# Four fifths of a layer's end moved from the turn between two batches to beside the last scans

## The chip, the cores and the metric

One core of one Trainium2 chip. TensorE is PE (its weight loads PEld), VectorE is DVE, ScalarE is ACT, GpSimd is POOL, SyncE is SP. The granted clock is the share of TensorE's full speed that the profile records as allowed.

## The reference, cut to what matters

Four images of 48 x 48 tokens with 128 channels. Layer 0 is a group norm, an input projection to 256 + 256 channels, a depthwise convolution, a selective scan in four directions, and the "layer's end": layer norm over 256 channels, gate, output projection, residual. Layer 1 is attention over the 2304 tokens and then an STU (a causal convolution with 16 spectral filters, and 2 x 16 matrices that are a mixture of four sets).

```python
xz = einsum('bhwc,ec->bhwe', _gn(x), in_proj_w); xin, z = split(xz, 2)
xc = silu(conv(xin) + conv_b)
xs = stack([rows, columns, rows reversed, columns reversed])        # 4 directions, L = 2304
... dt, B, C from xs
h = h * exp(dt*A) + (dt*u)*B;  y = sum_n h*C                        # scan, d = 256, n = 16
y = sum of the four directions, put back in order of rows
y = (y - mu) * rsqrt(var + 1e-5) * norm_g + norm_b                  # over 256 channels
x = x + (y * silu(z)) @ out_proj_w.T                                # the layer's end
t = x; t = t + attention(_ln_t(t)); t = t + stu(_ln_t(t))
```

## The kernel before

One batch is a **scan stage** and a **turn**. The scan stage is 4 directions x 6 chunks of 384 positions; a chunk is 8 "units" (2 halves of the channels x 4 quads of states), so 192 units. Per unit, ACT makes four exponentials, DVE four scans, POOL the product with C, PE the sum over states (y) and the spreading of B over partitions, and DVE or POOL the input product.

```python
# order of the chunks: rows, columns, rows reversed, columns reversed
order = [(k, c) for k in range(K) for c in (range(NCH) if k < 2 else reversed(range(NCH)))]
...
def scans(b, chunks, preps, front, sp, back, work, work_cols):
    total = len(chunks) * CHUNK_COLS + work_cols        # matmul columns of the stage
    def more(share):
        while done[0] < share * total:                  # filler: STU of batch b-1,
            cols = next(work, None)                     # for batch 0 the mixture
            if cols is None: break
            done[0] += cols
    for s in range(len(units) + 2):
        enter(s)                                        # input product s = rep * B
        units[s].scan(0, back.psa); units[s - 1].times_c(); units[s].scan(1, back.psa)
        prepare(s)                                      # a step of the next chunk's preparation
        more((s + 0.5) / len(units))
        spread(s + 2)                                   # B of a coming unit, on PE
        units[s].scan(2, back.psa); units[s].scan(3, back.psa)
        ...
        units[s - 2].sum_c(back.psy)                    # y, on PE
        more((s + 1) / len(units)); prepare(s)
```

PE takes its instructions in this order. The mixture, the filler of batch 0, loads its matrices where it uses them:

```python
def mixture(pool, ps):                                  # pool.two: two buffers
    for k in range(KF):
        M = [pool.two.tile(...) for j in range(2)]
        for t, src in zip(M, ("M_phi_plus", "M_phi_minus")):
            nc.sync.dma_start(t, a[src][:, k].rearrange("i d e -> d i e"))
        ... matmuls on M, yielding after each
```

The layer's end works on five pieces of the tokens (four of 512, one of 256) in pipelined stages, after all scans, with the attention's first slots and a part of the next batch's prologue beside it:

```python
def means(J):    # PE: mean over channels; ACT: zr = Silu(zr)
def center(J):   # DVE: v = v - mu (PSUM), twice; ACT: square
def gate(J):     # DVE: v = v * zr (both in SBUF), twice; POOL: sum of squares
# then: project and variance (PE), add to the residual T (DVE), layer norm to xn (DVE, ACT, POOL),
#       transposes to xnT (PE, ACT)

for b in range(B):
    scans(b, ...)                                        # scan stage
    for i, J in enumerate(epilogue(b, ...)):             # layer's end
        if i % 2 and parts: parts.pop(0)()               # prologue of batch b+1
        if J is not None: next(at) ...                   # attention slots of that piece
    for i in range(slots - BEGIN): next(at); ...         # attention, prologue
    ...                                                  # exp/ln table; first chunk of batch b+1
# after the last batch: its STU alone
```

## Time and profile before

7157.76 us, median of 3 runs (7152.87 to 7163.85). The span of the profiled run is 7140.9 us. A scan stage runs from the batch's first scan to its last y product, a turn from there to the next batch's first scan (the last turn: to the first transfer of the last STU).

| before, us | batch 0 | 1 | 2 | 3 |
|---|---|---|---|---|
| scan stage | 1073.7 | 1343.8 | 1349.3 | 1333.5 |
| last y product to first attention score | 86.7 | 86.8 | 87.9 | 71.9 |
| turn | 308.2 | 308.3 | 309.5 | 236.1 |

The rows below are the view of engine busy time by stretch of the kernel before: stretch and length, then busy time and records of PE, PEld, DVE, ACT and POOL, then the granted clock, the DMA share and GB/s.

```profile
126.90:1200.60 1073.70, 800.85 (x3085) 326.02 (x3085) 949.57 (x980) 642.72 (x1196) 930.54 (x425) 0.75 0.55 132
1508.80:2852.60 1343.80, 1271.18 (x5777) 728.68 (x5777) 1075.96 (x1305) 617.95 (x1177) 932.81 (x424) 0.98 0.68 174
2604.00:2852.60 248.60, 226.88 (x1289) 151.83 (x1289) 166.16 (x212) 85.33 (x172) 149.34 (x65) 0.93 0.60 168
```

Length is PE busy plus PE idle, and that sum is used throughout. Batch 1's stage is 1271 busy + 73 idle at a clock of 0.98: PE-bound. Batch 0's has PE at 75% and DVE and POOL at 87 to 88%. The last row, the end of batch 1's stage, is PE-bound like the rest: PE is busy 227 of 249 us there and DVE 166.

### The profile page before, as it was taken

The page shows a single profiled execution, that of the slowest core. Times are in us where ns is not written, and L with a number is a line of the kernel's source. Part 1 is how long each engine was busy: PE and PEld are TensorE (multiplying, and loading weights), DVE is VectorE, ACT ScalarE, POOL GpSimd, SP SyncE. Part 2 cuts the span into 40 slices and gives each one's busy share as a digit, 9 for nine tenths or more (in the row PEclk, how much of TensorE's full clock was granted, in tenths as well). Part 3 has the DMA queues.
Part 4 walks back from the last instruction along what each step waited for, and adds up shares of the span by engine and source line. Part 5 has one row for each costly group of instructions (what it writes and reads, how often), then busy time and mean ns, then how long its engine had stood idle before and what let it go on. Part 6 is the DMA issues. An engine that isn't in the chain of part 4 may idle for free. (4 is left out here: it accounts for less than half of the span.)

```text
span 7140.9 us, 79677 instructions
## 1 busy us (share of the span) xinstructions
PE 6335.6 (89%) x26760; PEld 3652.2 (51%) x26760; DVE 4863.0 (68%) x6145; ACT 2986.6 (42%) x5616; POOL 3849.3 (54%) x1815
## 2 busy tenths in 40 slices
PE   4777776888999998778999999788999999789999
PEld 2333333434555565534555556534555556547788
DVE  6898897557888876457888886447888887522111
ACT  3666664334445543334454543234454544231000
POOL 2888886036777765126677775205677776300000
PEclk7777777899999999899999999899999999899999
DMA  3555553046777765135767776125676777215545
GB/s 95 139 136 137 135 140 98 22 116 151 177 180 187 190 186 166 37 89 138 173 183 181 189 186 194 44 60 139 168 181 175 196 181 205 83 41 139 159 139 177
DMA packets 648922, 1019.14 MB, mean 143 GB/s; under 512 B 93849, under 2 KB 506649, under 8 KB 623778
## 3 DMA queue, kind: packets, MB, share of 16 engines
q1 hardware_dynamic: 642816, 1010.84, 54.3%
q8 instruction: 213, 3.49, 0.2%
q10 hardware_dynamic: 5698, 3.21, 0.2%
q14 instruction: 195, 1.60, 0.1%
HBM read 895.86 MB, written 117.84 MB: 142 GB/s over the span
## 5 line engine op out<-in xcount | busy, mean ns | idle before, releaser
L456 POOL TENSOR_TENSOR s<-s,bc 128x1536 f32<-128x1536 f32 x768 | 2645.1, 3445 | 260.5 <-DVE s L447 160.2
L447 DVE TENSOR_TENSOR_SCAN s<-dA,carry,s 128x384 f32<-128x384 f32 x2560 | 2440.0, 1001 | 253.5 <-ACT dA L444 251.8
L444 ACT ACTIVATE dA<-rep,A 128x384 f32<-128x384 f32 x3072 | 1753.1, 584 | 973.9 <-DVE s L447 956.2
L939 PE MATMUL cv<-tt,u 128*128 128x256 f32 (+4 forms) x7680 | 1686.6, 359 | 59.4 <-DVE U L959 39.8
L939 PEld LDWEIGHTS cv<-tt,u 128*128 128x128 f32 (+1 forms) x7680 | 1272.3, 191 | 670.2 <-issue 335.7
L959 DVE TENSOR_TENSOR U<-cv,Q 128x256 f32<-128x256 f32 (+1 forms) x1280 | 494.0, 392 | 1035.5 <-PE cv L939 1021.6
L439 POOL TENSOR_TENSOR s<-rep,bc 128x1536 f32<-128x1536 f32 x288 | 993.3, 3449 | 97.7 <-DMA bc<-bcd 97.7
L939 PE MATMUL cv<-tt,us 128*128 128x256 f32 (+4 forms) x3840 | 870.7, 363 | 78.9 <-DVE U L959 41.0
L439 DVE TENSOR_TENSOR s<-rep,B 128x1536 f32<-128x1536 f32 x480 | 834.5, 1739 | 100.6 <-PE B L431 84.6
L464 PE MATMUL y<-s,csum 128*32 128x384 f32 x6144 | 716.2, 541 | 169.1 <-POOL s L456 154.4
L939 PEld LDWEIGHTS cv<-tt,us 128*128 128x128 f32 (+1 forms) x3840 | 637.3, 192 | 321.5 <-issue 96.2
L948 ACT COPY Q<-cv 128x256 f32<-128x256 f32 (+3 forms) x640 | 224.0, 351 | 1377.9 <-PE cv L939 1242.3
L997 PE MATMUL pr<-U,G 128*128 128x512 f32 (+4 forms) x2048 | 717.6, 482 | 48.7 <-DMA G<-gd 40.5
L455 POOL COPY carry<-s 128x4 f32<-128x4 f32 x640 | 120.5, 188 | 1132.9 <-DVE s L447 1049.5
L431 PE MATMUL B<-xd,spread 32*128 32x384 f32 x960 | 475.0, 576 | 18.0 <-DVE s L439 18.0
L447 DVE TENSOR_TENSOR_SCAN s<-dA,s 128x384 f32<-128x384 f32 x512 | 457.1, 940 | 39.2 <-ACT dA L444 37.8
L997 PEld LDWEIGHTS pr<-U,G 128*128 128x128 f32 x2048 | 339.0, 194 | 251.6 <-issue 147.8
L464 PEld LDWEIGHTS y<-s,csum 128*32 128x32 f32 x6144 | 125.5, 111 | 603.4 <-issue 301.8
L700 PE MATMUL s<-xnT 128*128 128x512 f32 (+1 forms) x720 | 356.0, 580 | 51.8 <-ACT e L702 28.5
L702 ACT ACTIVATE e<-s,shift 128x512 f32<-128x512 f32 (+1 forms) x360 | 231.4, 644 | 335.2 <-PE s L700 335.0
L161 POOL TENSOR_TENSOR ln_vu<-ln_vu,mhalf 128x4 f32<-128x4 f32 (+1 forms) x20 | 31.4, 1571 | 623.1 <-DVE ln_vu L160 623.1
L693 PE MATMUL o<-e,xn 128*128 128x512 f32 (+1 forms) x720 | 340.2, 556 | 0.0
(167 smaller groups left out, 4883.4 us busy)
## 6 DMA issues: line engine op xcount, KB each, us to landing
rep<-dtdud SPq DMA_DIRECT2D x768, 384.0 KB, 7.8
tt<-fd SPq DMA_DIRECT2D x192, 577.0 KB, 4.2
bc<-bcd SPq DMA_DIRECT2D x2304, 48.0 KB, 3.7
tt<-fd SPq DMA_DIRECT2D x192, 513.0 KB, 4.2
tt<-fd SPq DMA_DIRECT2D x192, 385.0 KB, 3.8
dtdud<-re SPq DMA_DIRECT2D x768, 96.0 KB, 2.2
G<-gd SPq DMA_DIRECT2D x192, 256.0 KB, 4.8
tt<-fd SPq DMA_DIRECT2D x64, 514.0 KB, 5.4
```

The costliest lines, as they stand in the source:

```text
L431: nc.tensor.matmul(self.bt[:, :CS], spread[32:64, self.q].rearrange("p c j -> p (c j)"), self.ch.xd[32:64], start=True, stop=True)
L439: eng.tensor_tensor(s, self.ch.rep[self.h][:, 1], bt.unsqueeze(1).to_broadcast([P, G4, CS]), ALU.mult)
L444: nc.scalar.activation(dA[:, :CS], ch.rep[self.h][:, 0, g], AF.Exp, scale=A[:, ch.k, self.h * G4 + g, self.q:self.q + 1])
L447: nc.vector.tensor_tensor_scan(s, dA[:, CS - 1::-1] if ch.rev else dA[:, :CS], s, 0.0 if ch.first else carry[:, self.h, self.q, g:g + 1], ...
L456: nc.gpsimd.tensor_tensor(self.s, self.s, ch.bc[Q4 + self.q].unsqueeze(1).to_broadcast([P, G4, CS]), ALU.mult)
L464: nc.tensor.matmul(ch.y[g * DL:(g + 1) * DL, :CS], csum, self.s[:, g], start=(self.q == 0), stop=(self.q == Q4 - 1))
L693: nc.tensor.matmul(po[J][:, :w], xn[:, i], e[:, :w], start=(i == 0), stop=(i == NT - 1))
L700: nc.tensor.matmul(p[:, :w], xnT[:, i * P:(i + 1) * P], xnT[:, 512 * J:512 * J + w], start=True, stop=True)
L702: nc.scalar.activation(e[:, :w], p[:, :w], AF.Exp, bias=shift)
L939: nc.tensor.matmul(p2[:, :, at - first:], x, t[:kp, :, hi - 1 - at + J * P:end if end >= 0 else None:-1], start=(J == 0), stop=(J == nb - 1))
L959: nc.vector.tensor_tensor(dst, src, q, ALU.add)
L997: nc.tensor.matmul(p[:, :, :v], Gs[n][:, q, x, :], U[n][:, 4 * q:4 * q + 4, :v], start=False, stop=(k == KF - 1 and q == 1 and v == w))
```

## The change

Intent: the turn begins with the layer's end, in which PE idles and no other engine is full. If the last direction is the one along the rows, backwards, then the rows are complete from the end as its chunks finish, and four of five pieces (the last rows first) could be done while the last scans still run. Their buffers are taken not to fit beside the STU's, so the STU (the mixture for batch 0) is issued within the first 84% of the units, its buffers are freed, and the pieces come after it. Silu is replaced by tanh in the prologue, to stay in one table set.

```diff
-    order = [(k, c) for k in range(K) for c in (range(NCH) if k < 2 else reversed(range(NCH)))]
+    order = [(k, c) for k in (0, 1, 3, 2) for c in (range(NCH) if k < 2 else reversed(range(NCH)))]
 # prologue, for z:
-                    nc.scalar.copy(t, now["ps"][:, :SUB])
+                    nc.scalar.activation(t, now["ps"][:, :SUB], AF.Tanh)      # win's z half is halved
+                    nc.vector.scalar_tensor_tensor(t, t, 1.0, now["ps"][:, :SUB], ALU.add, ALU.mult)
 # scans:
+    WORK_END = 0.84
-        total = len(chunks) * CHUNK_COLS + work_cols
+        total = WORK_END * len(chunks) * CHUNK_COLS + work_cols
-            while done[0] < share * total:
+            while done[0] < share / WORK_END * total or share > WORK_END:
                 cols = next(work, None)
                 if cols is None:
+                    late(complete[0])                  # one step of the pieces
                     break
+        def add_y(u):                                  # notes down to which row y is complete
 # epilogue() becomes class Finish, piece(J) a generator of 11 to 12 steps:
 #   load z, T | mean | centre, square | gate, sum of squares | project 0, variance |
 #   rsqrt, project 2 | add 0 | add 2, norm | norm | norm | transpose | copy
+        def steps():
+            for J in range(NM - 1, 0, -1):             # pieces 4, 3, 2, 1; piece 0 in the turn
+                while now[0] > 512 * J // CS: yield
+                for _ in fin[b].piece(J, bank, vbank): yield
 # attention starts with what is ready:
-        pieces = [0, 4, 1, 2, 3]
+        pieces = [1, 4, 2, 3, 0]
+        keys = [*range(PIECES[0], NT), *range(PIECES[0])]
 # (cut: PSUM and SBUF pools, piece 0 interleaved with attention, exp_tanh() at the turn)
```

## The prediction

> **What bounds the kernel now.** One batch is one scan stage (24 chunks of 384 positions times 8 quads, 192 "units", with the previous batch's STU as PE filler; the mixture of the STU's matrices as filler for batch 0), then one "turn" (the layer's end in five pieces, attention, the prologue of the next batch). After the last turn the last STU runs alone. I read the engine shares by slice first, then cut the span at the first scan and the first mean matmul of each batch in the view of engine busy time by stretch. Columns: stretch, its length, busy time (and records) of PE, PEld, DVE, ACT, POOL, then granted clock, DMA share, GB/s.
>
> ```profile
> 199.00:1200.50 1001.50, 753.24 (x2924) 304.57 (x2922) 900.68 (x927) 607.75 (x1131) 877.77 (x401) 0.75 0.56 133
> 1508.80:2870.80 1362.00, 1284.31 (x5818) 737.66 (x5819) 1082.64 (x1314) 624.44 (x1185) 934.60 (x425) 0.97 0.68 175
> 3160.90:4510.20 1349.30, 1276.05 (x5777) 732.53 (x5777) 1076.01 (x1305) 617.93 (x1177) 932.45 (x424) 0.97 0.67 173
> 4819.70:6153.20 1333.50, 1262.85 (x5776) 723.31 (x5776) 1075.61 (x1305) 620.26 (x1179) 930.92 (x423) 0.98 0.68 177
> 6404.80:7141.00 736.20, 730.80 (x3452) 578.99 (x3452) 128.84 (x323) 58.26 (x163) 0.00 (x0) 1.00 0.50 152
> ```
>
> The reader is to see two regimes. Batch 0's scans take 1001 us, 5.2 us a unit, with DVE and POOL near full and PE at 75%. The other three take 1348 us on average with PE busy 1274 us of it. The last row says what an STU costs PE by itself: 731 us. So in those three stages PE has 731 of STU and 1274 - 731 = 543 of scan work: PE sets their end, while DVE could go at batch 0's pace. Slices of 50 us from the middle and the beginning of the third such stage:
>
> ```profile
> 5560.00:5610.00 50.00, 50.00 (x228) 29.52 (x225) 43.98 (x52) 25.48 (x47) 39.16 (x19) 1.00 0.72 192
> 4910.00:4960.00 50.00, 37.41 (x137) 17.32 (x136) 33.08 (x44) 17.39 (x36) 26.28 (x13) 0.93 0.59 137
> ```
>
> PE is saturated in the middle; most of its idle time, 30 of 71 us, lies in the first 190 us of the stage (waits for G transfers and for DVE to empty PSUM). DVE in batch 0 is closer to full than its 90% says: only 726 of its 768 scan records are in the trace there. In the third PE-bound stage, where all 768 are, DVE is busy 1076 us, less about 117 for the STU's U additions, so 5.0 us a unit against the 5.2 us that a unit takes. The turn of batch 2, cut at the first score matmul and at the table load for the next scans:
>
> ```profile
> 4510.20:4598.10 87.90, 60.12 (x234) 50.18 (x230) 43.73 (x100) 14.82 (x24) 16.21 (x16) 0.71 0.16 53
> 4598.10:4737.20 139.10, 123.79 (x339) 63.06 (x340) 69.48 (x81) 59.76 (x106) 7.37 (x9) 0.93 0.08 26
> 4737.20:4819.70 82.50, 62.76 (x154) 26.45 (x152) 23.54 (x41) 30.97 (x50) 6.93 (x3) 0.91 0.36 85
> ```
>
> Row one is the layer's end: 88 us with PE 60 us busy at a clock of 0.71. It is 87, 69, 88 and 72 us in the four batches. This is what the change goes after.
>
> **What the Trainium skill says.** "SBUF — State Buffer", section "Who interferes with whom": a DVE instruction with two SBUF inputs contends with a GpSimd instruction that reads SBUF, and the later of the two blocks for the whole of the other. The trace agrees (start, duration, instruction):
>
> ```profile
> 1496.85 3.42 POOL L439 TENSOR_TENSOR s<-rep,bc 128x1536 f32<-128x1536 f32 x1
> 1496.92 3.90 DVE L163 TENSOR_TENSOR u<-u,ln_vu 128x512 f32<-128x512 f32 x1 [1.18 <-POOL ln_vu L161]
> 1209.59 2.38 DVE L615 TENSOR_TENSOR ya<-ya,zr 128x512 f32<-128x512 f32 x2 [4.42 <-ACT sq L609]
> 1218.88 1.28 DVE L615 TENSOR_TENSOR ya<-ya,zr 128x512 f32<-128x512 f32 x2
> ```
>
> The normalising product of L163 takes 0.69 us elsewhere; started 0.07 us after a 3.42 us POOL product it took 3.90, and ended with it. The pair of gate products took 2.38 us beside a POOL addition and 1.28 us alone. "TensorE: Matmul & The Clock Gate", section "What's actually happening": the clock is granted by how busy PE has lately been; here 0.71 to 0.75 where PE idles and 0.97 to 1.00 where it doesn't. "ScalarE: Activation LUTs", section "Table sets: the hidden batching unit": exp and tanh share a set. The loads in this trace take 1.28 us each; dropping the Silu set in each turn is worth about that, four times, some 5 us in all at most.
>
> **The change part by part.**
>
> *Silu by tanh in the prologue.* 12 copies a batch become tanh (same size, some 0.48 us each), and 12 DVE operations from PSUM are added; by L470's 0.68 us for the same shape, 8 us of DVE a prologue, in a stretch where DVE is half idle. Removed: 5 Silus of about 0.96 us a batch. About zero on the path.
>
> *The order of directions.* Last is the direction along rows, backwards, so the rows are complete from the end. Same instructions, zero. It opens the gate: piece 4 after the fifth-last chunk, piece 1 when only the last 8 units remain. A piece has 11 to 12 steps, two a unit, so 4 pieces fit the last 31 units.
>
> *The STU squeezed into 84% of the units.* The first 161 units now carry all 731 us of STU. The last 31 units have little PE work: 31 x 1.44 us (y 0.87 and 5/8 of B at 0.93) = 45, and 2.5 chunk preparations of about 10 us = 25; sum 70. So the first part needs PE 1274 - 70 = 1204 us, and with 50 of the old 71 us of idle time kept (its cause, the first blocks, is kept), about 1254. The last 31 units then go at the pace of batch 0: 31 x 5.2 = 161. Together 1415 against 1348: +67 for each of three stages. This price is certain in kind: work that two engines could share over the whole stage is now bound first by PE, then by DVE.
>
> *Four of five pieces beside the last scans.* DVE per piece of four: 2 centrings at 0.63, 2 gates at 0.66, 4 scaled adds at 0.34, 2 adds at 0.42, and 3.2 for the layer norm and the reciprocal root = 8.0 us; 3.5 such pieces are 28 us. In these units DVE is the bound, so nearly all of it, 26 us, lengthens the stage. POOL gets 3.5 x 3.5 = 12 us, with room. PE gets 43 us (14/18 of 55), into its gap: free.
>
> *The turn.* The layer's end of 69 to 88 us goes, except piece 0 (12 us of PE, now beside attention), 8 us of prologue PE work that lay in it and now lengthens the 139 us stretch (which is PE-bound, 124 of 139), and about 6 us of drain and waits. Gains 61, 43, 62 and 53 (no prologue in the last): 219 us in all.
>
> *Sum without contention.* Batch 0: its filler has room, so +26 - 61 = -35. Batches 1 to 3: 3 x (67 + 26) - 158 = +121. In all +86 us.
>
> **The rivals.**
>
> *A: the lock.* Beside the last scans POOL is about 80% busy with products that read SBUF. Each piece has four wide DVE operations with two SBUF inputs (two gates, two of the norm) and two tiny ones (L160 reached 0.62 us instead of 0.17, so they block too). At 0.8 x half of 3.4 us each, some 8 to 10 us a piece, 30 to 35 a batch, all on the engine that is the bound: +130 in all, so about +215. For it: the rows above. Against: some of it falls into DVE's other waits.
>
> *B: PE bursts.* Projection and variance of a piece are some 6 us of PE at a low clock in one step, and the B product of a coming unit stands behind them; in batch 0, DVE waited 29 us for B behind the mixture. A few us a piece, up to 40 in all.
>
> *C: the change as intended.* STU denser means fewer waits of PE for DVE, and the first part could run without idle time: 1204 instead of 1254, three times, -150; with the pieces hidden in DVE's waits, a result near -100. For it: PE does reach 100% in the middle, and who wrote it will have chosen 0.84 by trying. Against: the waits at the beginning of the stage are for transfers and for the emptying of PSUM, which a denser STU does not shorten.
>
> *D: one step too late.* If piece 1 is not through when the scans end, attention starts behind it: 10 to 20 us a turn.
>
> **Range and chances.** My sum says +86 and with the lock +215; C pulls to -100. I weight C at about a third, since a tuned constant speaks for someone having seen a gain, and arrive at +70: **7230 us**. 8 times in 10 between **7100 and 7380**. A gain over 2% (below 7015) would need C whole and more: 0.03. Slower by over 2% (above 7301) is the sum with most of the lock: 0.29. Within 2%: 0.68.
>
> **What would show it.** Right: the mean matmul of piece 4 about 30 units before the end of the scans; the first score matmul within 10 us of the last y product, where it was 69 to 88; the scan stages of batches 1 to 3 longer by 80 to 130 us, PE busy below 75% and DVE above 95% in their last 190 us; batch 0's stage longer by 25 to 60; gate products with durations of 2 to 4 us and the POOL product ending together with them; no Silu table load. Wrong: if the first 161 units take under 1220 us, the idle time I kept was not kept (C); if the gates take 0.66 us in the late units, the lock (A) is not there; if the turn shrinks by less than 40 us, attention was held by something other than the layer's end, such as the prologue's DVE work or piece 1 (D).

## More of the kernel before

The metric is the device time of one execution in microseconds (us).

The STU after the last turn takes 751.5 us.

## The result, and the profile after

The changed kernel takes **7402.19 us** (median of 4 runs, 7400.12 to 7424.5) against 7160.51 for the kernel before in the same rounds: ratio 1.0346, 95% interval 1.0324 to 1.0368, slower. Ratios here are the mean time of one kernel's runs over that of the other's in the same rounds, so they differ a little from the ratio of the medians.

The turn did become shorter. The two rows of the page that show the slices, for the kernel after (tenths busy of PE, tenths of the granted clock):

```profile
PE   4777776879999997778999998788999999689999
PEclk7777776989999997889999997789999998699999
```

A slice is 185 us. The clock has its dips to 6 and 7 at slices 6, 15, 24 to 25 and 34 (counted from 0), with PE's share falling in the same places: there the four scan stages now end. By the same cuts as before:

| after, us | batch 0 | 1 | 2 | 3 | sum, after - before |
|---|---|---|---|---|---|
| scan stage | 1168.1 | 1489.6 | 1474.9 | 1487.4 | +519.6 |
| last y to first score | 3.4 | 3.0 | 3.0 | 3.5 | |
| turn | 241.7 | 242.1 | 242.1 | 171.8 | -264.4 |

With +4.4 before the first scan and +0.1 in the last STU the sum is +259.7, the whole difference of the two profiled runs (7140.9 to 7400.6). So attention now starts 3 us after the last y product, the turns give 66 us each, and the scan stages take twice that away. The stages of batches 0 and 1 of the kernel after, cut in two at the filler's last instruction on PE, and batch 1's turn:

```profile
131.30:1084.80 953.50, 716.70 (x2713) 303.40 (x2713) 797.25 (x821) 552.34 (x1043) 773.28 (x356) 0.74 0.55 131
1084.80:1299.40 214.60, 137.47 (x543) 64.00 (x543) 192.32 (x225) 97.14 (x171) 172.19 (x86) 0.67 0.39 94
1541.10:2818.40 1277.30, 1209.52 (x5418) 713.67 (x5422) 931.55 (x1151) 534.32 (x1033) 783.33 (x358) 0.97 0.66 170
2818.40:3030.70 212.30, 134.82 (x534) 64.25 (x533) 189.86 (x219) 91.56 (x162) 164.13 (x82) 0.66 0.39 93
3030.70:3272.80 242.10, 203.94 (x553) 102.58 (x552) 114.35 (x166) 90.11 (x155) 16.64 (x12) 0.92 0.17 47
```

What the reader is to see: the first part of batch 1 (row 3) is as PE-bound as the whole stage was before, 1210 busy and 68 idle. The last part (row 4) has turned into a second regime: PE busy 135 of 212 us at a clock of 0.66, DVE busy 190. Together PE is now idle 145 us of the stage instead of 73, and busy 1344 instead of 1271.

What fills DVE in those 212 us, as groups of instructions of the kernel after (count, busy us, mean ns, idle us before them):

```profile
L621 DVE TENSOR_TENSOR ya<-ya,ez 128x512 f32<-128x512 f32 (+1 forms) x8 | 12.9, 1654 | 0.0
L156 DVE TENSOR_SCALAR ln_sa<-ln_sa 128x4 f32<-128x4 f32 (+1 forms) x4 | 7.9, 1978 | 0.1
L638 DVE SCALAR_TENSOR_TENSOR T<-op,rd,T 128x128 f32<-128x128 f32 x14 | 4.1, 334 | 0.0
L157 DVE TENSOR_TENSOR xn<-T,ln_sa 128x512 f32<-128x512 f32 (+1 forms) x4 | 2.5, 626 | 0.1
```

The gates (L621; six of 512 columns and two of 256) average 1654 ns; the six wide ones alone average 1784 ns, where the undisturbed pair in the prediction took 1.28 us, 0.64 each. The scaling of four (once two) numbers per partition (L156) averages 1978 ns. The timeline of the kernel after (start, duration, instruction) shows a pair of gates meeting a POOL product:

```profile
2865.82 4.65 DVE L621 TENSOR_TENSOR ya<-ya,ez 128x512 f32<-128x512 f32 x2
2866.05 3.87 POOL L441 TENSOR_TENSOR s<-rep,bc 128x1536 f32<-128x1536 f32 x1
```

The pair takes 4.65 us. The POOL product, issued 0.23 us later, takes 3.87 instead of 3.45 and ends at 2869.92; the pair ends at 2870.47. So the first gate went first and the second waited for POOL: the lock of the prediction's rival A.

In batch 0 the waits by engine and releaser (total us, times, longest us), from 126 to 1090 us; the first block is the kernel before, the second the kernel after:

```profile
PE G L812 <- DMA M<-in_M_phi_plus: 107.1, 15, 15.5
```

```profile
PE G L830 <- DMA M<-in_M_phi_plus: 138.2, 16, 15.7
...
DVE s L449 <- ACT dA L446: 57.4, 28, 12.6
DVE s L441 <- PE B L433: 32.7, 8, 13.6
DVE ya L472 <- PE y L466: 25.4, 5, 13.3
```

PE stands still for the mixture's matrices M, up to 15.7 us at a time, sixteen times, and DVE's longest waits (12.6 to 13.6 us, for the exponentials, B and y) are of nearly that length: what is behind M on PE is what DVE needs next.

### The profile page after: what moved, and what is told of

Read it like the earlier page. It is cut to its first block, busy times and chain, and to the rows that moved or that the text cites.

```text
span 7400.6 us, 79730 instructions
## 1 busy us (share of the span) xinstructions
PE 6438.7 (87%) x26760; PEld 3693.9 (50%) x26760; DVE 4951.5 (67%) x6194; ACT 2955.1 (40%) x5592; POOL 3853.3 (52%) x1815
## 4 chain that ended last, share of the span: by engine, by line
PE 59%; DVE 21%; DMA 9%; issue 3%; ACT 3%; POOL 2%; SPq 2%; DVEq 0%; ACTq 0%; POOLq 0%
PE cv L957 25%; DVE s L449 11%; PE pr L1015 7%; PE y L466 5%; PE sp L397 4%; DVE s L441 4%; PE B L433 3%; PE s L718 3%; DMA tt<-fd 3%; PE o L711 3%; DMA G<-gd 2%; DMA rep<-dtdud 2%; DVE xc L268 2%; PE dt L366 2%; PE xp L356 1%
## 5 line engine op out<-in xcount | busy, mean ns | idle before, releaser
L957 PE MATMUL cv<-tt,u 128*128 128x256 f32 (+4 forms) x7680 | 1661.4, 357 | 54.8 <-DVE U L977 41.6
L466 PE MATMUL y<-s,csum 128*32 128x384 f32 x6144 | 753.8, 568 | 203.3 <-POOL s L458 137.9
L433 PE MATMUL B<-xd,spread 32*128 32x384 f32 x960 | 503.9, 608 | 45.1 <-DVE s L441 45.1
L830 PE MATMUL G<-M,W 128*128 128x128 f32 (+2 forms) x768 | 235.8, 459 | 138.2 <-DMA M<-in_M_phi_plus 138.2
```

The lines of the kernel that those rows point to most:

```text
L433: nc.tensor.matmul(self.bt[:, :CS], spread[32:64, self.q].rearrange("p c j -> p (c j)"), self.ch.xd[32:64], start=True, stop=True)
L466: nc.tensor.matmul(ch.y[g * DL:(g + 1) * DL, :CS], csum, self.s[:, g], start=(self.q == 0), stop=(self.q == Q4 - 1))
L830: nc.tensor.matmul(p[:, :n] if j else p[:, NF - 1 - i], W[:, q if t else 0, i], M[t][:, i].unsqueeze(1).to_broadcast([P, n, C]) if j else ...
L957: nc.tensor.matmul(p2[:, :, at - first:], x, t[:kp, :, hi - 1 - at + J * P:end if end >= 0 else None:-1], start=(J == 0), stop=(J == nb - 1))
```

## The experiments

Theory after the result: two losses, one from the squeeze of the filler and one from DVE work (with the lock) added where DVE had become the bound; and in batch 0 the waits for M. Rivals: that order and tanh cost something by themselves, that nearly all of the loss is the lock, or that the placing of the pieces is wrong and the squeeze harmless. Eleven kernels ran, all with correct results. They ran in four groups (a to d, e to h, i and j, k), each with the kernel before in the same rounds; across groups the ratios compare better than the medians.

| run | median us | ratio to before (95%) |
|---|---|---|
| a: order and tanh | 7165.98 | 1.0016 (1.0007 to 1.0024) |
| b: a and squeeze to 0.84 | 7414.41 | 1.0378 (1.0352 to 1.0404) |
| c: after, less lock | 7370.23 | 1.0317 (1.0298 to 1.0336) |
| d: after, M ahead | 7312.02 | 1.0229 (1.0210 to 1.0248) |
| e: after, 0.94 | 7313.22 | 1.0201 (1.0165 to 1.0236) |
| f: pieces beside the STU | 7213.39 | 1.0067 (1.0048 to 1.0087) |
| g: before, M ahead | **7108.97** | 0.9914 (0.9893 to 0.9936) |
| h: f, M ahead | 7165.21 | 1.0007 (0.9997 to 1.0017) |
| i: a and squeeze to 0.94 | 7319.75 | 1.0207 (1.0183 to 1.0230) |
| j: after, less lock, M ahead | 7257.49 | 1.0133 (1.0107 to 1.0159) |
| k: a, five s buffers | 7166.44 | 1.0014 (1.0006 to 1.0022) |

### a: order and tanh alone

```diff
 # kernel before, with
+    order ... for k in (0, 1, 3, 2)
+    tanh and scalar_tensor_tensor in place of the copy of z; Silu dropped; exp_tanh() at the turn
```

> The kernel before with only the new order of directions and Silu by tanh; the layer's end stays whole after the scans, and the STU spreads over all units. Theory 1 (the price is the squeeze of the filler): the time of before, 7160 within 20 us. Rival (the backward row order or the 12 more DVE operations of the prologue cost something): above 7200 us.

7165.98 us, ratio 1.0016, as expected: some 11 us of the loss by the ratio, 13 by the medians. The rest is squeeze and pieces.

### b: the squeeze without the pieces

```diff
 # a, with
+    WORK_END = 0.84      and its two lines in scans(); the layer's end stays in the turn
```

> The run above plus the filler squeezed into 84% of the units; the layer's end stays after the scans. Theory 1: batches 1 to 3 each longer by some 105 us (the first part as in the changed kernel, 1272 us, then 31 units at about 5.1 us and the drain), batch 0 by some 40 to 60 us (the mixture's stalls closer together); about 7160 + 370 = 7530 us, slower than the changed kernel. Rival (the loss comes from the pieces among the scans, through the shared port or the order of the queues): near 7200 us.

7414.41 us. That is as slow as the whole change (7402.19), so pieces and turn together come out at about -12 us, less than the spread of b's runs (7401 to 7444), and **the squeeze is the loss**. The rival that it is nearly free falls; the size expected, some 100 us more, was too high. Its four stages take 1119.3, 1435.1, 1430.7 and 1416.6 us. Batch 1's stage of this kernel, the same two parts:

```profile
1557.20:2839.50 1282.30, 1218.10 (x5418) 722.53 (x5421) 931.79 (x1151) 534.42 (x1033) 783.28 (x358) 0.96 0.65 169
2839.50:2992.30 152.80, 91.11 (x364) 24.98 (x363) 146.25 (x154) 85.05 (x145) 148.31 (x66) 0.66 0.46 105
```

DVE is busy 146 of 153 us in the second row: the last 31 units (4.9 us each) are DVE-bound, with PE idle 62 us there. Sum for the stage, compared with before: PE busy 1218 + 91 = 1309 (before 1271, +38) and idle 64 + 62 = 126 (before 73, +53), so +91. The idle time is the filler that is missing. The extra busy time has the same work in it (5782 matmul records, before 5777), most of it at the lower clock of row two, 0.66 instead of 0.98: a y matmul averages 765 ns there and 508 in the stage before. But DVE bounds that part, so I do not read the lower clock as what makes it long: at a higher one PE would idle there for longer. The first part was not quickened by being dense: its 64 us of idle time nearly equal the 73 us of the whole stage before.

Subtracting b from the kernel after, stage by stage, gives the price of the pieces among the scans: 48.8, 54.5, 44.2 and 70.8 us, 218 in all. The turns give 264. (b's profiled run was the slowest of its four, 7444 against a median of 7414, so the 218 may be some 30 too low, which is the difference to the -12 us of the medians.) In batch 1's last part it is 153 to 212 us: DVE busy 146 to 190 and DVE waiting 7 to 22.

### c: the lock taken out where it can be

The centred values stay in PSUM, so that the gate has only one input in SBUF, and the small scaling goes to ACT.

```diff
 # kernel after, with
+            cen = [bank(f"cen{b}_{J}")[:, :w], mu]
-                nc.vector.tensor_tensor(y[h], y[h], mu, ALU.subtract)
+                nc.vector.tensor_tensor(cen[h], y[h], mu, ALU.subtract)      # result in PSUM
-                nc.vector.tensor_tensor(y[h], y[h], z[:, h], ALU.mult)
+                nc.vector.tensor_tensor(y[h], cen[h], z[:, h], ALU.mult)
 # normed():
-        nc.vector.tensor_scalar_mul(s, s, 1.0 / C)
+        nc.scalar.activation(s, s, AF.Copy, scale=1.0 / C)
```

> The changed kernel with the gate products reading the centred values from PSUM (one SBUF input) and the scaling of the mean done by ScalarE. In the changed kernel's trace the eight gate products beside the scans take 12.9 us where 5 would do, and the four scalings 7.9 where 0.7 would: theory (the shared port blocks them, on the engine that bounds those units): gates near 0.7 us each, 10 to 15 us less a batch, 7402 - 50 = about 7350 us. Rival (DVE has room there, the waits are hidden): 7402 within 10 us.

7370.23 us: 32 us better than the kernel after, 20 less than expected. All four runs (7361 to 7388) lie below all four of the kernel after (7400 to 7425), but the ratios to the kernel before, 1.0317 and 1.0346, have intervals that just overlap: the sign is well supported, the size is not. The groups of DVE in the last part of batch 1 of this run:

```profile
L157 DVE TENSOR_TENSOR xn<-T,ln_sa 128x512 f32<-128x512 f32 (+1 forms) x4 | 8.3, 2075 | 1.1 <-ACT ln_sa L156 1.1
L622 DVE TENSOR_TENSOR ya<-mu,ez 128x512 f32<-128x512 f32 (+1 forms) x4 | 2.5, 618 | 0.0
L622 DVE TENSOR_TENSOR ya<-cen,ez 128x512 f32<-128x512 f32 (+1 forms) x4 | 2.4, 602 | 0.0
```

Gates with one input in PSUM take 0.61 us instead of 1.65: the lock was real there. But with the tiny scaling gone from DVE, the subtraction behind it (L157, both inputs in SBUF) went from 626 to 2075 ns. This fits the reading that it had been fast before because the scaling in front of it had sat out the POOL product. DVE's busy time in that part fell from 190 to 179.4 us, and the part from 212 to 204.

### d: M loaded one step ahead

```diff
 # mixture(), kernel after
+        nxt = load_M(0)
         for k in range(KF):
-            M = [...]; dma_start(...)
+            M, nxt = nxt, load_M(k + 1)         # same two buffers
```

> The changed kernel with the mixture's two M matrices loaded one step ahead. In batch 0 PE stands 138 us before its first product with a fresh M, and DVE idles 158 us in the first part. Theory (PE in order, held by M, holds B and y and with them the scans; squeezed together this costs more): first part of batch 0 from 954 to 830 to 880 us, the whole to about 7310 us. Rival (batch 0 is bound by the pace of DVE and POOL and the squeeze itself is the cause): 7402 within 20 us.

7312.02 us, 90 better than the kernel after, as expected. One of the sixteen waits is left, the first, and batch 0's first part took 847.5 instead of 953.5 us:

```profile
PE G L836 <- DMA M<-in_M_phi_plus: 15.5, 1, 15.5
```

```profile
134.20:981.70 847.50, 693.02 (x2713) 293.73 (x2713) 794.71 (x822) 553.03 (x1043) 773.61 (x356) 0.78 0.62 148
```

So a good part of batch 0's loss, which my prediction had as 26 us, comes from a wait that its filler brings with it. Run g shows how much of that wait the kernel before has already paid.

### e: the kernel after, with the filler ending at 0.94

```diff
-    WORK_END = 0.84
+    WORK_END = 0.94
 # step():
             next(gen, None)
+            next(gen, None)                      # two steps a call, so that four pieces still fit
```

> The changed kernel with the STU's end at 94% of the units instead of 84%, and two steps of a piece at each call instead of one, so that the four pieces still fit. Theory (the loss grows with the number of units that run without filler): squeezing alone cost 261 us at 16% of the units, so about 100 at 6%, and the pieces about what the turn gives back: near 7250 us, 150 us faster than the changed kernel. Rival (the pieces among the scans cost it): no faster than 7350, since the same pieces now stand closer together.

7313.22 us, runs from 7277.57 to 7337.7. Better than 0.84 by 89 us, less than the theory of a price in proportion to the units without filler had it (7250), more than its rival. Run i asks the same of the squeeze alone.

### i: the squeeze alone, ending at 0.94

```diff
 # b, with
-    WORK_END = 0.84
+    WORK_END = 0.94
```

> The squeeze alone, as in the second run, but to 94% of the units instead of 84%. Theory (the loss is the idle time of PE while units run without filler): with 11.5 instead of 31 such units, about 40% of the 261 us: some 105 us, 7260 us. Rival (a fixed cost of the denser filler, as in batch 0's mixture, or of the emptying of the queue at the switch): most of the 261 us stays, 7350 or more.

7319.75 us, so +161 us over the kernel before of its own rounds (7158.51), against b's +261 (over 7152.95). Only 6% of the units are without filler instead of 16%, and the price is 62% of b's: it lies between the two expectations, and neither was met. Against e (7313.22) the pieces and the shorter turns again come out at about nothing, as they did at 0.84. Batch 1's two parts:

```profile
1544.20:2875.70 1331.50, 1263.43 (x5653) 733.33 (x5653) 1022.54 (x1249) 593.66 (x1133) 879.00 (x404) 0.97 0.67 173
2875.70:2935.70 60.00, 26.70 (x125) 5.41 (x125) 53.84 (x56) 27.29 (x46) 53.39 (x20) 0.58 0.24 54
```

PE busy 1263 + 27 = 1290 (+19) and idle 68 + 33 = 101 (+29) come to +48 over batch 1 before, whose stage is the same work. The end without filler costs PE 33 us of idle time in 60 us, a higher rate than b's 62 in 153, and the clock falls to 0.58. The price per unit is thus highest in the very last units: 48 us for the last 11.5, and 43 more (b's 91) for the 19.5 before them.

The early part keeps its idle time whether it is 1277, 1331 or, with no squeeze, 1344 us long. The traces show where much of it lies. The first 190 us of batch 1's stage, first of the kernel before, then of the kernel after:

```profile
1508.80:1698.80 190.00, 162.49 (x596) 78.55 (x597) 139.41 (x182) 80.56 (x159) 110.59 (x55) 0.94 0.62 147
1541.10:1731.10 190.00, 159.48 (x574) 81.02 (x574) 128.30 (x173) 72.61 (x144) 101.23 (x50) 0.92 0.58 133
```

PE idles 28 and 31 us there (32 in b, 29 in i): a denser filler does not take away what a stage loses at its beginning. That the transfers and PSUM waits named in the prediction are its cause was not tested; no run took them away.

### f: the pieces beside the STU, no squeeze

If the squeeze is the loss, the pieces should be run without it. They then have to live beside the STU's buffers: kept whole in SBUF they did not fit (a first build ended with SBUF full; this rests on my word), which would also explain why the change waits for the STU's end. So the pieces were reduced to 6 KB, their results go through DRAM and come back in the turn, and the PSUM bank is the one of the chunk preparations, when none holds it.

```diff
 # kernel after, with
-    WORK_END = 0.84
+    WORK_END = 1.0
+            if not any(pend.values()): late(complete[0])     # in prepare(): bank is free
 # Finish: tiles z and sq reused for squares, tokens, normed tokens and transposes (6 KB);
 #   T, xn, xnT stored to DRAM piece by piece, loaded at the turn; no step keeps a bank
-        sp = Stage(tc, f"h{b}", "left", s=(6, SB))
+        sp = Stage(tc, f"h{b}", "left", s=(5 if b else 6, SB))
```

> No squeeze: the STU spreads over all units as before, and the four pieces run among the last quarter of the scans beside it. For that the pieces use the PSUM bank of the chunk preparations, each step giving it back at once, and only 6 KB of SBUF each: their results go to DRAM and are loaded again in the turn; batches 1 to 3 have 5 instead of 6 buffers for s. Theory (in a stretch that PE bounds, a piece costs its 43 us of PE a batch and its DVE time is hidden; the turn gives back some 60): about 17 us gained in each of batches 1 to 3 and about 10 in batch 0: 7153 - 60 = some 7090 us. Rival (a piece among scans costs some 59 us wherever it stands, by waits of engines in order): 7140 or more.

7213.39 us, ratio 1.0067. The rival was right: it loses too. The turns are short (241.2, 244.7, 244.6 and 173.2 us), but the stages are 72, 86, 75 and 88 us longer. Batch 1's stage and its last 248 us:

```profile
1518.00:2947.80 1429.80, 1333.93 (x5947) 778.39 (x5947) 1113.00 (x1374) 628.58 (x1194) 940.38 (x436) 0.95 0.66 168
2700.00:2948.00 248.00, 216.72 (x1103) 151.49 (x1102) 145.93 (x200) 71.44 (x140) 122.42 (x57) 0.83 0.50 146
```

Busy 1334 (+63 over before), idle 96 (+23). The groups of the pieces' own matmuls sum to 47 us (mean 8, variance 6, projection 30, transposes 3); the rest I put down to the clock, without a test: 0.95 instead of 0.98 over the stage and 0.83 instead of 0.93 in its last 248 us. PE is the bound in this stage, so the pieces are not beside it but on it. This is not a pure test: steps that run from PE to DVE and back within one step tie the two together, and the round trip through DRAM is its own. It shows that this placing costs more than it saves, not that every placing must. With run e against i and the kernel after against b, the pieces were moved in three ways here (filler to 100%, 94% and 84%): +47, -6 and -12 us by the medians, +36, -4 and -23 by the ratios. None paid clearly.

### g, h: M ahead in the kernel before and in f

```diff
 # mixture() of the kernel before (g), of f (h): load_M one step ahead, as in d
```

> The kernel before with only the mixture's M matrices loaded one step ahead. In its batch 0 PE stands 114 us before M and DVE idles 120 us. If M held the scans there too: about 100 us less, 7050 us. If M held them only when squeezed: 7153 within 20 us.

> The kernel with the pieces between scans without a squeeze, plus M one step ahead. If the two are independent: the sum of their gains, about 6990 us. If batch 0, then bound by DVE alone, pays the pieces in full, some 30 to 40 us more: up to 7030 us.

g: **7108.97 us** (7089.66 to 7113.77), ratio 0.9914, faster than both kernels. Batch 0's stage fell from 1073.7 to 1019.5 us and the waits for M from 107.1 to 15.4:

```profile
PE G L818 <- DMA M<-in_M_phi_plus: 15.4, 1, 15.4
```

```profile
126.50:1146.00 1019.50, 794.34 (x3085) 323.82 (x3085) 948.60 (x980) 643.39 (x1196) 930.44 (x425) 0.76 0.59 139
```

92 us of waits gone and 54 us of time won: so with the filler spread over all units a part of the waits was not on the path. In the squeezed kernel (run d) the same edit took away 123 us of waits and won 106 us of batch 0's stage. With M ahead in both, that stage takes 1062.2 us in d and 1019.5 in g, so 43 of the 94 us that the change had cost batch 0 remain, near the 49 of the pieces. Of the 106 us that M costs in the squeezed kernel, the kernel before had paid 54 already; the other 52, about half of batch 0's loss, came with the squeeze. I had expected 7050, or no gain; it is half. h: 7165.21 us, 48 better than f, so again batch 0 alone, and no better than the kernel before. The expectation (below 7030) failed by f's cost in the other batches, which this edit does not touch.

### j: the mends of c and d together

```diff
 # kernel after, with the edits of c and of d
```

> The changed kernel with both mends, the products freed of the shared port (alone 32 us) and M one step ahead (alone 90 us). If they are independent: 7402 - 122 = 7280 us, still over 100 us slower than the kernel before, because PE's idle time behind the squeeze in batches 1 to 3 stays. If the lock mattered only through batch 0's stalls: 7310.

7257.49 us: 145 us better than the kernel after, about as much as c's 32 and d's 90 together (the runs of one kernel spread over 20 to 40 us). Nothing shows that they share a cause. What is left over the kernel before is a ratio of 1.0133. In batch 1 the stage is still 130 us longer (1474.2), of which the squeeze alone has 91 in run b, and the turn gives back 68.

### k: control for f

```diff
 # a, with
+        sp = Stage(tc, f"h{b}", "left", s=(5 if b else 6, SB))
```

> A control for the kernel with the pieces between scans: the first run's kernel (new order, Silu by tanh) with 5 instead of 6 buffers for s in batches 1 to 3, nothing else. If the missing buffer were what made the stages of batches 1 to 3 longer there: some 80 us a batch, 7400 us. If the pieces themselves did: 7166 within 20 us.

7166.44 us against a's 7165.98: without the pieces the missing sixth buffer costs nothing, so it alone does not make f's loss.

## Why the prediction was wrong

The range ended at 7380 and the chance for slower was 0.29; it is 7402 and slower.

- **The step that failed is the weight given to rival C at the end**, that is to a wait that was to vanish: PE's idle time in the first 161 units. The runs showed that it stays. Those units took 1277, 1263 and 1276 us, not under 1220, with 61 to 68 us of idle time in each (50 assumed in the sum, none in C): C is refuted by the prediction's own mark. The sum of the prediction's own terms with the lock was "about +215", that is 7373; measured is +242, and +260 in the profiled runs. The +70 comes out as two thirds of the middle of +86 and +215, less a third of 100. C pulled it down by 83 us, with the reason that "a tuned constant speaks for someone having seen a gain". That was not read from the profile, and what the profile offered spoke against C (the waits at the stage's beginning). Even C's -100 is not the sum of its terms, which is 86 - 150 - 104 = -168.
- **That +215 came near is partly luck.** Its terms are off in both directions: squeeze 201 predicted and 301 measured in b's profile (which is 30 above b's median), pieces with the lock 234 and 218, turns -219 and -264. The squeeze is the term that was too small.
- **Squeeze, batches 1 to 3.** Predicted +67 a stage by the two-regime sum 1254 + 161. Run b measured +91, +81 and +83: first part 1282 and last part 153 in batch 1. The mechanism was right. The mis-sized term is the first part: 1282 and not 1254, because it kept 64 us of idle time (50 assumed) and PE was busy 1218 (1204 assumed, from a stage at a clock of 0.98; here it was 0.96). PE's work in the last 31 units, put at 70 us, measured 91 at a clock of 0.66; at the busy time per instruction of the stage before it would be some 72, my estimate, so the count of work was right. That error did not lengthen the stage, since DVE bounds those units: they took 153, a little less than my 161.
- **Batch 0.** The term "its filler has room, so +26" was wrong: +94, of which b has 46 as the squeeze's and 49 are the pieces'. The squeeze, priced at nothing here, was the missing term. My cut at 199 us started the stage 72 us late, and "5.2 us a unit" and the 42 missing scan records follow from that: all 768 scans are in the trace from 126.9, 5.6 us a unit. The waits for M, which the trace of the kernel before shows as 107 us, I saw only as "DVE waited 29 us for B"; they are what a denser filler makes dearer (run d won 106 us of the stage, run g only 54 without the squeeze).
- **Pieces.** 26 us of DVE work a stage, "nearly all of it" on the bound: DVE's work was 28 us, as it turned out, and the lock added 15 (gates 12.9 us where about 5 are due, scalings 7.9 instead of 0.7), half of the 30 to 35 that rival A gave, so that counting the lock half was about right. But the last part grew by 59 us in batch 1, since DVE also waited 22 us there instead of 7. Of that wait I can say where it is (exponentials 6.3 us, y and variance 5.3, B 2.2; none of these in run b) and not which of PE's bursts caused which; rival B named it, and it stays open.
- **The turn.** Predicted 219 us in four turns, measured 264, 66 each. The first score does start 3 us after the last y product; D did not happen. The 69 us for batch 1's layer's end was a cut at 2870.8 where it should have been 2852.6: it is 87.
- **The marks.** Piece 4's mean matmul came at 2819.8, 31 units before the end. PE was at 64% in the last part (under 75, right), DVE at 89% (above 95, wrong), the gates were blocked, the Silu table load is gone. Batches 1 to 3 lengthened by 146, 126 and 154, two of the three above the 80 to 130, and batch 0 by 94, above the 25 to 60. One reading of the prediction was loose: the 3.90 us product of L163 did not end with the POOL product but 0.55 us after it (1500.82 against 1500.27), having waited for it.

## What to carry to other kernels

Filler that lets two engines overlap was worth most in this kernel where it was spread evenly: pressing it into 84% of the units cost more than the gap at the end of the stage was worth, because the part with it stays bound by one engine and the part without it is bound by another. Before moving work beside a stage, ask which engine bounds that stage and add the moved work to that engine, with any lock it brings; and when a sum read from the profile and an argument about someone's tuning disagree, keep the sum, and check it term by term. Look at the filler itself too: the gain here, 0.9% for one load a step earlier, lay in a wait the kernel had had all along.

## What the Trainium skill lacked or had wrong

- "SBUF — State Buffer", section "Who interferes with whom", states the lock between DVE instructions with two SBUF inputs and POOL. The runs agree: gates 1654 ns on average beside POOL, 0.61 us with one input in PSUM. It does not say that taking one such instruction away lets the next one block: the subtraction went from 626 to 2075 ns when the scaling before it was moved to ACT.
- The same section lists a scaling by a constant among the instructions that can take the shared ports, without a size. Here even one of 128 x 4 or 128 x 2 values was held up: three of the four in batch 1's last part took 1.88 to 2.98 us and ended within 0.05 us of the end of a POOL product, and the fourth, with POOL idle, took 0.17. An instruction of three inputs, one of them in PSUM and one a scalar per partition, was not blocked (334 ns on average; a pair took 0.58 us beside a POOL product and 0.60 with POOL idle); the section does not name that form.
- "TensorE: Matmul & The Clock Gate", section "What's actually happening", has the clock follow PE's recent activity. The runs agree (mean granted clock 0.58 at 45% busy, 0.66 at 64%, 0.95 to 0.98 above 93%), but the page's examples are gaps in which matmuls wait, for transfers above all, and none is of filler taken out: that lengthened the remaining matmuls too, here from an estimated 72 to 91 us in the last 31 units of run b, though DVE, not PE, set their time.
